# An adapter with a residual and a layer norm on one core: x written ahead of a product, b2 moved between engines, and the order of work set by keys

## The chip, the cores and the metric

The kernel runs on one core of one Trainium2 chip. The metric is the device time of one execution in microseconds (us), the median of several. A core has a TensorE (matmul; the profile lists its weight loads apart as PEld), a VectorE (DVE), a ScalarE (ACT), a GpSimd (POOL) and a SyncE (SP), which here issues DMAs. Each engine works through its own queue in order; semaphores hold one back until another has done its part. SBUF is the working memory, PSUM the memory that TensorE writes, in 8 banks of 128 x 512 float32.

## The reference

128 batches, each with x of 128 x 512 float32 and one id out of 10 that picks its weights:

```python
h = relu(x @ W1[id] + b1[id])            # 128x512 @ 512x128
adapted = h @ W2[id] + b2[id]            # 128x128 @ 128x512
y = x + adapted
normed = (y - mean(y)) * rsqrt(var(y) + 1e-5)
out = x + normed * gamma[id] + beta[id]
```

Everything is float32.

## The kernel before

One batch fills the 128 partitions, with x's 128 rows on them. All of W1 (`w1`), W2 (`w2`), and beta, gamma and b2 spread over the partitions (`beta_b`, `gamma_b`, `b2_b`) lie in SBUF; an id, read into a register by `lid`, picks a slice of 512 columns. For each batch:

- TensorE transposes x in four pieces into `pxT` (`transpose_x`, L271), multiplies by W1 in four steps into `ph` ("down", L294), and by W2 into `py` ("up", L311). A float32 product stands as two matmuls in the profile.
- ScalarE copies `pxT` to `xT` (`copy_xT`, L275), applies relu with b1 (`relu`, L302, `ph` to `hT`), copies the W1 of a coming batch into a tile of its own (`stage_w1`, L262; for batches 0 to 16 a DMA does that by id), and squares y with its sum kept (`square`, L351, followed by a read of the accumulator). Once for each pair of batches it makes the negative means (`scalar_means`, L342) and the first reciprocal root (`deviation`, L361).
- GpSimd adds beta to x (`add_beta`, L288, into the output tile `o`) and b2 to x (`add_b2`, L281, into `r`).
- VectorE adds `r` to `py` in place with the row sums kept (`residual`, L328), refines the root in three small steps a pair (`rstd`, L365, L367, L370), then forms (y - mean) * gamma (`scale`, L394), and times the deviation plus `o` (`finish`, L403). SP stores a pair (`store`, L407).

For 27 of the batches b2 is not added by GpSimd: VectorE adds it to `py` (`vector_b2`, L321) ahead of a residual that reads x itself. For batches 0, 1, 126 and 127 a small matmul adds it.

PSUM: `pxT`, `ph` and the roots have one bank each, `py` has five, used in turn; so the bank of batch b is that of batch b - 5, free after the latter's `finish`. x comes in groups of four batches (`load_x`, four tiles), `r` has four tiles, `o` eight of a pair each.

The order on each engine is the order in which the program calls the steps (`keep` chains each instruction to the one before it on its engine). After a start written out by hand, a loop over i from 3 to 121 calls, in one turn: the transposes of batch i, the adds of GpSimd for batch i - 1, the product down, xT copy and relu around batches i and i - 1, the W1 copy of batch i + 1, the product up of batch i - 2, and VectorE's and ScalarE's statistics for batch i - 3 and the pair before it. The last batches from 121 on (E = B - 5 = 123) are again written out by hand, step for step.

Of the kernel before, what the change touches and what calls it, by code (L numbers as in the profile page):

```python
# [8 lines left out]
FP = mybir.dt.float32  # L9
# [7 lines left out]
P = 128  # L17
# [3 lines left out]
EARLY = 17  # L21
LATE = 17
U = 2


@with_exitstack
def cond_resid_kernel(ctx: ExitStack, tc: tile.TileContext, x, itok, W1, b1, W2, b2, gamma, beta, out):
# [41 lines left out]
    def load_x(g):  # L69
        t = xp.tile([P, G, H], FP, tag="x", name=f"x_{g}")  # L70
        keep(nc.sync.dma_start(out=t, in_=x[g * G : (g + 1) * G].rearrange("b s h -> s b h")))
        xs[g] = t

    def xb(b):
        return xs[b // G][:, b % G, :]
# [64 lines left out]
    def lid(b, engine):  # L140
        g = b // G
        if (g, engine) not in lids:
            loads, vals = nc.values_load_multi_w_load_instructions(  # L143
                lang[0:1, g * G : (g + 1) * G],
                engines=[engine],
                min_val=0,
                max_val=L - 1,
                skip_runtime_bounds_check_because="clamped on the chip to 0..L-1 above",
            )
            for ins in loads:  # L150
                keep(ins)
            lids[g, engine] = vals
        return lids[g, engine][b % G]
# [99 lines left out]
    def b2_by_matmul(b):  # L253
        return b in (0, 1) or b >= B - 2

    def b2_by_vector(b):
        return b in (2, 3, 9, 13, 17, 21) or 24 <= b < B - 8 and (b % 16 in (1, 6, 11) or b % 32 == 30)

    def stage_w1(b):
        w1s[b] = wp.tile([P, KC, A], FP, tag="w1s", name=f"w1s_{b}")  # L260
        src = w1.rearrange("p l k a -> p (l k a)")[:, bass.ds(lid(b, ET.Activation) * (KC * A), KC * A)]
        keep(nc.scalar.copy(w1s[b].rearrange("p k a -> p (k a)"), src))  # L262

    def transpose_x(b):
        pxs[b] = p_x.tile([P, KC, P], FP, tag="xT", name=f"pxT_{b}")
        for k in range(KC):
            if b < EARLY:
                cols = xb(b).rearrange("s (p k) -> s k p", k=KC)[:, k, :]
            else:
                cols = xb(b)[:, k * P : (k + 1) * P]  # L270
            keep(nc.tensor.transpose(pxs[b][:, k, :], cols, ident))  # L271

    def copy_xT(b):
        xT[b] = tp.tile([P, KC, P], FP, tag="xT", name=f"xT_{b}")
        keep(nc.scalar.copy(xT[b], pxs.pop(b)))  # L275

    def add_b2(b):
        if not b2_by_matmul(b) and not b2_by_vector(b):
            rs[b] = rp.tile([P, H], FP, tag="r", name=f"r_{b}")
            v = lid(b, ET.Pool)  # L280
            keep(nc.gpsimd.tensor_tensor(rs[b], xb(b), b2_b[:, bass.ds(v * H, H)], ALU.add))  # L281

    def add_beta(b):
        g, j = divmod(b, 2)
        if j == 0:
            os[g] = op.tile([P, 2, H], FP, tag="o", name=f"o_{g}")
        v = lid(b, ET.Pool)
        keep(nc.gpsimd.tensor_tensor(os[g][:, j, :], xb(b), beta_b[:, bass.ds(v * H, H)], ALU.add))  # L288

    def down(b):  # L290
        phs[b] = p_h.tile([P, P], FP, tag="h", name=f"ph_{b}")
        for k in range(KC):
            keep(
                nc.tensor.matmul(  # L294
                    phs[b], lhsT=w1s[b][:, k, :], rhs=xT[b][:, k, :], start=(k == 0), stop=(k == KC - 1)
                )
            )
        del xT[b], w1s[b]

    def relu(b):  # L300
        hT[b] = tp.tile([P, P], FP, tag="hT", name=f"hT_{b}", bufs=6)
        keep(nc.scalar.activation(hT[b], phs.pop(b), AF.Relu, bias=b1T[:, bass.ds(lid(b, ET.Activation), 1)]))  # L302

    def up(b):
        v = lid(b, ET.PE)
        ys[b] = p_y.tile([P, H], FP, tag="y", name=f"py_{b}")
        m = b2_by_matmul(b)
        if m:
            pick_b = pick[:, bass.ds(v + 2 * L, 1)].to_broadcast([96, P])
            keep(nc.tensor.matmul(ys[b], lhsT=pick_b, rhs=parts[:96, :], start=True, stop=False))  # L310
        keep(nc.tensor.matmul(ys[b], lhsT=hT[b], rhs=w2[:, bass.ds(v * H, H)], start=not m, stop=True))  # L311
        del hT[b]

    def col(tiles, b):

        return tiles[b // 2][:, b % 2 : b % 2 + 1]

    def vector_b2(b):
        if b2_by_vector(b):
            v = lid(b, ET.DVE)  # L320
            keep(nc.vector.tensor_tensor(ys[b], ys[b], b2_b[:, bass.ds(v * H, H)], ALU.add))  # L321

    def residual(b):
        r = rs.pop(b) if b in rs else xb(b)
        if b % 2 == 0:
            sums[b // 2] = st.tile([P, 2], FP, tag="sum", name=f"sum_{b // 2}")
        keep(
            nc.vector.scalar_tensor_tensor(ys[b], ys[b], 1.0, r, ALU.mult, ALU.add, accum_out=col(sums, b))  # L328
        )

    def negative_means(g):
# [12 lines left out]
    def square(b):  # L344

        g, j = divmod(b, 2)
        if j == 0:
            ssqs[g] = st.tile([P, 2], FP, tag="ssq", name=f"ssq_{g}")
        sq = tp.tile([P, H], FP, tag="sq", name=f"sq_{b}")
        keep(  # L350
            nc.scalar.activation(  # L351
                sq, ys[b], AF.Square, bias=col(sums, b), scale=-float(H), accum_out=col(ssqs, b)
            )
        )
# [24 lines left out]
    def deviation(g):  # L379
        root(ssqs[g], of_pair(g)[0])  # L380

    def rstd(g, n):
        t, u = of_pair(g)
        if n < 3:
            newton(n, ssqs[g], t, u)
        else:
            rstds[g] = st.tile([P, 2], FP, tag="rstd", name=f"rstd_{g}")
            newton_3(rstds[g], t, u)
            del ssqs[g], parts_of[g]

    def scale(b):
        v = lid(b, ET.DVE)
        keep(
            nc.vector.scalar_tensor_tensor(  # L394
                ys[b], ys[b], col(nmeans, b), gamma_b[:, bass.ds(v * H, H)], ALU.add, ALU.mult
            )
        )

    def finish(b):
        g, j = divmod(b, 2)  # L400
        o = os[g][:, j, :]
        keep(
            nc.vector.scalar_tensor_tensor(o, ys[b], rstds[g][:, j : j + 1], o, ALU.mult, ALU.add)  # L403
        )
# [4 lines left out]
    def on(b):  # L409
        return 0 <= b < B  # L410
# [48 lines left out]

    def square_of(b):  # L460
        ssqs[-b] = st.tile([P, 1], FP, tag="ssq", name=f"ssq_of_{b}")
        sq = tp.tile([P, H], FP, tag="sq", name=f"sq_{b}")
        keep(nc.scalar.activation(sq, ys[b], AF.Square, bias=col(sums, b), scale=-float(H), accum_out=ssqs[-b]))

    def root_of(b):
# [112 lines left out]
    up(1)  # L578
    x_turn(4)

    turned = 5
    for i in range(3, B - 6):
        b = i - U - 1
        if b == 8 or b > 12 and b % G == 2 and b // G + 3 < NG:
            load_x(5 if b == 8 else b // G + 3)
        up_to = i
        if b <= E:
            if turned <= up_to and on(turned):
                transpose_x(turned)
            add_b2(b + 2)  # L590
            if 4 <= b + 2 <= E:
                add_beta(b + 2)
        for n in range(turned, min(B, up_to) + 1):
            if on(n) and (n > turned or b > E):
                transpose_x(n)
            down(n - 1)
            if on(n):
                copy_xT(n)
            relu(n - 1)
            if on(n + 1) and n + 1 >= FIRST:  # L600
                stage_w1(n + 1)
        turned = max(turned, min(B, up_to) + 1)
        if i - U >= 2 and on(i - U):
            up(i - U)

        g, half = divmod(b, 2)
        p = g - 1
        mine, old = 0 <= p < B // 2, 0 <= p - 1 < B // 2
        if half == 0:
            if on(b):  # L610
                vector_b2(b)
                residual(b)
                square(b)
            if mine:
                scale(2 * p)
                rstd(p, 1)
            if old:
                finish(2 * p - 1)
                store(p - 1)
        else:  # L620
            if on(b):
                vector_b2(b)
            if mine:
                rstd(p, 2)
            if on(b):
                residual(b)
                square(b)
            if mine:
                rstd(p, 3)
                scale(2 * p + 1)  # L630
            if mine:
                finish(2 * p)
        if 0 <= g and b <= E and half == 1:
            scalar_means(g)
            deviation(g)

        for n, engine in ((turned + 2, ET.Activation), (i - U + 3, ET.PE), (b + 1, ET.DVE), (b + 6, ET.Pool)):
            if on(n):
                lid(n, engine)

    lid(E - 3, ET.DVE)
    lid(E + 1, ET.DVE)
# [186 lines left out]
```

## Time and profile before

| | |
|---|---|
| time, median of 3 runs | 303.0 us (302.88 to 303.15) |
| profiled execution: span from first to last instruction | 301.3 us |
| what the median of the runs has above that span | 1.7 us |
| TensorE busy | 293.5 us, 97% |
| VectorE busy | 294.0 us, 98% |
| ScalarE busy | 278.5 us, 92% |
| GpSimd busy | 281.0 us, 93% |
| granted TensorE clock | 1.000 |
| moved by DMA | 78.11 MB, 259 GB/s |

The execution that was profiled has no other time than its span; the runs' times are those of executions as a whole. Busy times are sums of an engine's instructions, with overlaps counted once. Four engines are over 90% busy, so a share alone does not tell which of them sets the pace; that has to be read from the rows in order of time. In a row of the timeline the first number is the start, the second the duration, both in us; rows on one engine overlap, so what an instruction costs its engine is the distance from its start to the next one's start. Matmuls are pipelined, and their ends are modelled.

### The profile page before, as it was taken

To read this page: it belongs to the slowest core of one execution; us is meant where nothing else is said; L and a number is where in the kernel's file an instruction comes from. 1 tells how busy PE (TensorE), PEld (TensorE's weight loads), DVE (VectorE), ACT (ScalarE), POOL (GpSimd) and SP (SyncE) were. 2 spreads that over 40 slices of the span, in tenths; PEclk is the share of its full clock that TensorE was granted. 3 is DMA by queue.
4 is the path that set the end of the run, shared out by engine and by line. 5 is a ranking of instruction groups with operands and counts; after the bars stand their busy time and mean duration, and the time that the engine had idled before them with its cause. 6 is when DMAs were issued, how large, how long until landed. Compare 5 with 4: busy or idle time off the path is not lost.

```text
span 301.3 us, 7022 instructions
## 1 busy us (share of the span) xinstructions
PE 293.5 (97%) x1827; PEld 219.1 (73%) x1827; DVE 294.0 (98%) x785; ACT 278.5 (92%) x770; POOL 281.0 (93%) x236
## 2 busy tenths in 40 slices
PE   7899999999999999999999999999999999999993
PEld 3758787777777777777777777777777777777761
DVE  6989999999999999999999999999999999999996
ACT  5868789999999999999999999999999999999983
POOL 1299998999999999999999999999999999999982
PEclk9999999999999999999999999999999999999999
DMA  6999999996667776766687666668765767782826
GB/s 234 377 390 367 346 321 396 405 337 209 234 229 256 280 235 197 252 242 233 240 281 250 209 209 246 257 231 281 263 204 196 254 232 253 278 271 79 280 89 228
DMA packets 45353, 78.11 MB, mean 259 GB/s; under 512 B 2137, under 2 KB 9316, under 8 KB 45314
## 3 DMA queue, kind: packets, MB, share of 16 engines
q1 hardware_dynamic: 45254, 77.62, 74.9%
q8 instruction: 15, 0.25, 0.3%
q14 instruction: 24, 0.20, 0.2%
q10 hardware_dynamic: 60, 0.05, 0.1%
HBM read 44.11 MB, written 33.55 MB: 258 GB/s over the span
## 4 chain that ended last, share of the span: by engine, by line
PE 87%; DVE 5%; DMA 3%; issue 2%; SPq 1%; POOL 0%; DVEq 0%; POOLq 0%
PE ph L294 35%; PE py L311 35%; PE pxT L271 18%; DMA w<-in_L_cond_W_dram 3%; DVE py L328 1%; DVE o L488 1%; DVE py L394 1%; SPq L161 1%; DVE n L494 0%; SPq L143 0%; DVE rstd_of L370 0%; SPq L88 0%; DVEq L824 0%; DVE part_of L367 0%; DVE shift L434 0%
## 5 line engine op out<-in xcount | busy, mean ns | idle before, releaser
L288 POOL TENSOR_TENSOR o<-x,beta_b 128x512 f32<-128x512 f32 x121 | 158.4, 1331 | 12.8 <-DVE beta_b L247 11.6
L294 PE MATMUL ph<-xT,w1s 128*128 128x128 f32 x1024 | 135.4, 275 | 0.1
L311 PE MATMUL py<-w,hT 128*128 x256 | 131.5, 595 | 0.6 <-DMA w<-in_L_cond_W_dram 0.6
L294 PEld LDWEIGHTS ph<-xT,w1s 128*128 128x128 f32 x1024 | 124.9, 192 | 1.8 <-issue 0.8
L281 POOL TENSOR_TENSOR r<-x,b_b 128x512 f32<-128x512 f32 x92 | 122.7, 1334 | 0.0
L271 PEld LDWEIGHTS pxT<-ident,x 128*128 128x128 f32 x512 | 65.8, 149 | 66.3 <-issue 49.9
L394 DVE SCALAR_TENSOR_TENSOR py<-py,nmean,gamma_b 128x512 f32<-128x512 f32 x124 | 93.2, 752 | 0.0
L403 DVE SCALAR_TENSOR_TENSOR o<-py,rstd,o 128x512 f32<-128x512 f32 x116 | 86.5, 745 | 0.0
L351 ACT ACTIVATE sq<-py,sum 128x512 f32<-128x512 f32 x124 | 85.8, 692 | 0.2 <-DVE rstd L370 0.2
L275 ACT COPY xT<-pxT 128x512 f32<-128x512 f32 x128 | 74.7, 584 | 5.9 <-PE pxT L271 5.8
L271 PE MATMUL pxT<-ident,x 128*128 128x128 f32 x512 | 77.6, 274 | 0.9 <-ACT gamma_b L232 0.7
L328 DVE SCALAR_TENSOR_TENSOR py<-py,r 128x512 f32<-128x512 f32 x97 | 66.7, 688 | 0.1
L262 ACT COPY w1s<-w 128x512 f32 x108 | 66.2, 613 | 0.0
L302 ACT ACTIVATE hT<-ph,b1T 128x128 f32<-128x128 f32 x128 | 46.9, 367 | 8.6 <-PE ph L294 4.0
L311 PEld LDWEIGHTS py<-w,hT 128*128 128x128 f32 x256 | 39.0, 192 | 2.2 <-DMA w<-in_L_cond_W_dram 1.1
L351 ACT ACTIVATION_READ_ACCUMULATOR sq<-py,sum 128x1 f32 x124 | 25.1, 203 | 0.0
L328 DVE SCALAR_TENSOR_TENSOR py<-py,x 128x512 f32<-128x512 f32 x31 | 21.7, 699 | 0.8 <-PE py L311 0.3
L321 DVE TENSOR_TENSOR py<-py,b_b 128x512 f32<-128x512 f32 x27 | 18.6, 689 | 0.8 <-ACT xT L275 0.6
L361 ACT ACTIVATE root<-ssq,eps 128x2 f32<-128x2 f32 x62 | 16.4, 265 | 0.0
L328 DVE DVE_READ_ACCUMULATOR py<-py,r 128x1 f32 x97 | 13.4, 138 | 0.0
L342 ACT ACTIVATE nmean<-sum 128x2 f32<-128x2 f32 x61 | 12.1, 199 | 0.0
L370 DVE SCALAR_TENSOR_TENSOR rstd<-part,root 128x2 f32<-128x2 f32 x62 | 9.2, 149 | 0.0
(73 smaller groups left out, 104.5 us busy)
## 6 DMA issues: line engine op xcount, KB each, us to landing
out_dram<-o SPq DMA_DIRECT2D x62, 512.0 KB, 3.5
x<-in_x_dram SPq DMA_DIRECT2D x27, 1024.0 KB, 6.5
x<-in_x_dram SPq DMA_DIRECT2D x10, 512.0 KB, 6.0
w1s<-in_L_cond_W_dram SPq DMA_DIRECT2D x20, 256.0 KB, 7.7
w<-in_L_cond_W_dram SPq DMA_DIRECT2D x4, 640.0 KB, 8.4
w<-in_L_cond_W_dram SPq DMA_DIRECT2D x1, 1792.0 KB, 10.2
w<-in_L_cond_W_dram SPq DMA_DIRECT2D x1, 768.0 KB, 5.2
out_dram<-o SPq DMA_DIRECT2D x4, 128.0 KB, 1.7
```

Of the source, the lines that this page charges most:

```text
L262: keep(nc.scalar.copy(w1s[b].rearrange("p k a -> p (k a)"), src))
L271: keep(nc.tensor.transpose(pxs[b][:, k, :], cols, ident))
L275: keep(nc.scalar.copy(xT[b], pxs.pop(b)))
L281: keep(nc.gpsimd.tensor_tensor(rs[b], xb(b), b2_b[:, bass.ds(v * H, H)], ALU.add))
L288: keep(nc.gpsimd.tensor_tensor(os[g][:, j, :], xb(b), beta_b[:, bass.ds(v * H, H)], ALU.add))
L294: nc.tensor.matmul(phs[b], lhsT=w1s[b][:, k, :], rhs=xT[b][:, k, :], start=(k == 0), stop=(k == KC - 1))
L302: keep(nc.scalar.activation(hT[b], phs.pop(b), AF.Relu, bias=b1T[:, bass.ds(lid(b, ET.Activation), 1)]))
L311: keep(nc.tensor.matmul(ys[b], lhsT=hT[b], rhs=w2[:, bass.ds(v * H, H)], start=not m, stop=True))
L328: nc.vector.scalar_tensor_tensor(ys[b], ys[b], 1.0, r, ALU.mult, ALU.add, accum_out=col(sums, b))
L351: nc.scalar.activation(sq, ys[b], AF.Square, bias=col(sums, b), scale=-float(H), accum_out=col(ssqs, b))
L394: nc.vector.scalar_tensor_tensor(ys[b], ys[b], col(nmeans, b), gamma_b[:, bass.ds(v * H, H)], ALU.add, ALU.mult)
L403: nc.vector.scalar_tensor_tensor(o, ys[b], rstds[g][:, j : j + 1], o, ALU.mult, ALU.add)
```

## The change

The batches from 27 to 119 get a kind by their number modulo 16 (`KINDS`): 4 of 16 are E, 12 are P.

- P: GpSimd adds b2 to x, as before.
- E ("seeded"): ScalarE copies x into the batch's `py` bank (`seed`), the product up adds to what lies there (`start=False`), and VectorE's residual pass reads b2 in place of x or r. GpSimd does no b2 add.
- `vector_b2` is left for batches 2, 3, 9, 13, 17 and 21 alone.

Of the batches with number 13 modulo 16 from 29 to 109, six in all, W1 comes by a DMA by id (`load_late`) in place of ScalarE's copy.

The loop is replaced by a list: each step of each batch gets a key, in units of one batch, and the steps are called in the order of their keys. On ScalarE the W1 copy of a coming batch now mostly stands ahead of the relu, and a seed ahead of the xT copy of two batches later; on VectorE the last two of the three small steps follow each other directly in the middle. `EDGE` holds the keys of pairs outside the middle, `PAIR` those inside. `hT` has 5 tiles in place of 6, the squares' scratch tile 1 in place of 2. TensorE's order of matmuls, the start and the end written by hand stay.

```diff
+MIDDLE = 27
+TURNED = 19
+LAST = 8
+KINDS = 'EPPPPPEPPPEPEPPP'
+TURNS = 'TTTTTTTTTTTTTwTT'
+SEEDED = 'E'
+ON_GPSIMD = 'P'
+BATCH = dict(copy=0.09, r=0.59, beta=-0.52, relu=1.24, w1=-0.83, up=2.43, load=-4.76, r_late=-1.39)
+SEED = {'E': 1.88}
+PAIR = dict(stat=0.27, square=0.28, means=1.67, root=1.89, scale0=2.48, n1=2.77, n2=3.135, n3=3.19, scale1=3.02, end0=3.44, end1=4.28)
+EDGE = dict(stat=0.53, square=0.74, means=1.74, root=2.0, scale0=3.04, n1=2.84, n2=3.345, n3=3.7, scale1=4.07, end0=4.09, end1=4.71)
...
+    def kind(b):
+        return KINDS[b % len(KINDS)] if MIDDLE <= b < B - LAST else "-"
+
+    def turn(b):
+        return TURNS[b % len(TURNS)] if TURNED <= b < B - LAST - 2 else "-"
+
+    def seeded(b):
+        return kind(b) in SEEDED
...
     def b2_by_vector(b):
-        return b in (2, 3, 9, 13, 17, 21) or 24 <= b < B - 8 and (b % 16 in (1, 6, 11) or b % 32 == 30)
+        return kind(b) == "-" and (b in (2, 3, 9, 13, 17, 21) or 24 <= b < B - 8 and (b % 16 in (1, 6, 11) or b % 32 == 30))
...
+    def seed(b):
+        ys[b] = p_y.tile([P, H], FP, tag="y", name=f"py_{b}")
+        keep(nc.scalar.copy(ys[b], rs.pop(b) if b in rs else xb(b)))
...
-        hT[b] = tp.tile([P, P], FP, tag="hT", name=f"hT_{b}", bufs=6)
+        hT[b] = tp.tile([P, P], FP, tag="hT", name=f"hT_{b}", bufs=5)
...
     def up(b):
         v = lid(b, ET.PE)
+        if seeded(b):
+            cols = w2[:, bass.ds(v * H, H)]
+            keep(nc.tensor.matmul(ys[b], lhsT=hT[b], rhs=cols, start=False, stop=True, skip_group_check=True))
+            del hT[b]
+            return
...
     def residual(b):
-        r = rs.pop(b) if b in rs else xb(b)
...
+        if seeded(b):
+            r = b2_b[:, bass.ds(lid(b, ET.DVE) * H, H)]
+        else:
+            r = rs.pop(b) if b in rs else xb(b)
...
-        sq = tp.tile([P, H], FP, tag="sq", name=f"sq_{b}")
+        sq = tp.tile([P, H], FP, tag="sq", name=f"sq_{b}", bufs=1)
...
-    for i in range(3, B - 6):
...
+    for b in range(B):
+        if b >= 20 and b % G == 0:
+            at((11 if b == 20 else b - 7) - 0.01, load_x, b // G)
+        if b >= 3:
+            for n, engine in ((b + 5, ET.Activation), (b + 5, ET.PE), (b + 2, ET.DVE), (b + 6, ET.Pool)):
+                if on(n):
+                    at(b + 0.99, lid, n, engine)
+        if turn(b) in "Fw":
+            at(b + BATCH["load"] - 1, lid, b, ET.SP)
+            at(b + BATCH["load"], load_late, b)
+        if 5 <= b <= E - 2:
+            at(b, transpose_x, b)
+            at(b + BATCH["copy"], copy_xT, b)
+        if 4 <= b <= E - 3:
+            add_to = b + (BATCH["r"] if seeded(b) else BATCH["r_late"])
+            at(add_to, add_b2, b)
+            at(b + BATCH["beta"], add_beta, b)
+            at(b + 1.1, down, b)
+            at(b + BATCH["relu"], relu, b)
+        if seeded(b):
+            at(b + SEED[kind(b)], seed, b)
+        if FIRST <= b <= E - 1 and turn(b) not in "Fw":
+            at(b + BATCH["w1"], stage_w1, b)
+        if 2 <= b <= E - 4:
+            at(b + BATCH["up"], up, b)
...
+    for g in range(E // 2 - 1):
+        b = 2 * g
+        when = EDGE if "-" in (kind(b), kind(b + 2)) else PAIR
+        for j in (0, 1):
+            at_pair(g, j + when["stat"] - 0.01, vector_b2, b + j)
+            at_pair(g, j + when["stat"], residual, b + j)
+            at_pair(g, j + when["square"], square, b + j)
+        at_pair(g, when["means"], scalar_means, g)
+        at_pair(g, when["root"], deviation, g)
+        for n in (1, 2, 3):
+            at_pair(g, when[f"n{n}"], rstd, g, n)
+        for j in (0, 1):
+            at_pair(g, when[f"scale{j}"], scale, b + j)
+            at_pair(g, when[f"end{j}"], finish, b + j)
+        at_pair(g, when["end1"] + 0.001, store, g)
+
+    for _, _, step, args in sorted(plan, key=lambda step: step[:2]):
+        step(*args)
```

A step of a pair g gets the key 2g + 3 plus the number in `PAIR` or `EDGE` (`at_pair`); steps that the hand-written end does itself are left out of the list.

More of the change, by code (lines that the diff above doesn't have):

```diff
@@ L254, in b2_by_matmul, with b2_on_gpsimd, sum_of @@
         return b in (0, 1) or b >= B - 2
-    def b2_by_vector(b):
-        return b in (2, 3, 9, 13, 17, 21) or 24 <= b < B - 8 and (b % 16 in (1, 6, 11) or b % 32 == 30)
+    def kind(b):
[4 more added lines that the diff above has]
+        return kind(b) in SEEDED
+    def b2_on_gpsimd(b):
+        return kind(b) in ON_GPSIMD or kind(b) == "-" and not b2_by_matmul(b) and not b2_by_vector(b)
+    def b2_by_vector(b):
+        return kind(b) == "-" and (b in (2, 3, 9, 13, 17, 21) or 24 <= b < B - 8 and (b % 16 in (1, 6, 11) or b % 32 == 30))
+    def sum_of(b):
+        if b // 2 not in sums:
+            sums[b // 2] = st.tile([P, 2], FP, tag="sum", name=f"sum_{b // 2}")
+        return col(sums, b)
+    def seed(b):
+        ys[b] = p_y.tile([P, H], FP, tag="y", name=f"py_{b}")
+        keep(nc.scalar.copy(ys[b], rs.pop(b) if b in rs else xb(b)))
     def stage_w1(b):
@@ L277, in add_b2 @@
     def add_b2(b):
-        if not b2_by_matmul(b) and not b2_by_vector(b):
+        if b2_on_gpsimd(b):
             rs[b] = rp.tile([P, H], FP, tag="r", name=f"r_{b}")
@@ L323, in residual @@
     def residual(b):
-        r = rs.pop(b) if b in rs else xb(b)
-        if b % 2 == 0:
-            sums[b // 2] = st.tile([P, 2], FP, tag="sum", name=f"sum_{b // 2}")
+        if seeded(b):
+            r = b2_b[:, bass.ds(lid(b, ET.DVE) * H, H)]
+        else:
+            r = rs.pop(b) if b in rs else xb(b)
         keep(
-            nc.vector.scalar_tensor_tensor(ys[b], ys[b], 1.0, r, ALU.mult, ALU.add, accum_out=col(sums, b))
+            nc.vector.scalar_tensor_tensor(ys[b], ys[b], 1.0, r, ALU.mult, ALU.add, accum_out=sum_of(b))
         )
@@ L461, in square_of @@
         ssqs[-b] = st.tile([P, 1], FP, tag="ssq", name=f"ssq_of_{b}")
-        sq = tp.tile([P, H], FP, tag="sq", name=f"sq_{b}")
+        sq = tp.tile([P, H], FP, tag="sq", name=f"sq_{b}", bufs=1)
         keep(nc.scalar.activation(sq, ys[b], AF.Square, bias=col(sums, b), scale=-float(H), accum_out=ssqs[-b]))
@@ L579, in cond_resid_kernel @@
     x_turn(4)
-    turned = 5
-    for i in range(3, B - 6):
[L583 to L639, printed above, removed]
@@ new lines, in cond_resid_kernel, with at @@
+    plan = []
+    def at(when, step, *args):
+        plan.append((when, len(plan), step, args))
+    for b in range(B):
[23 more added lines that the diff above has]
+            at(b + BATCH["up"], up, b)
@@ new lines, in cond_resid_kernel, with at_pair @@
+    begun = [(step, n) for n in (E - 7, E - 6, E - 5) for step in (vector_b2, residual, square)]
+    begun += [(scalar_means, E // 2 - 3), (deviation, E // 2 - 3), (scale, E - 7), (rstd, E // 2 - 3, 1)]
+    def at_pair(g, when, step, *args):
+        if g < E // 2 - 3 or (step, *args) in begun:
+            at(2 * g + 3 + when, step, *args)
+    for g in range(E // 2 - 1):
[13 more added lines that the diff above has]
+        at_pair(g, when["end1"] + 0.001, store, g)
```

## Prediction

> **What bounds the kernel now.** I read the page's first part, then the chain that ended last, then the stages, then single rows of one steady stretch.
>
> ```profile
> span 301.3 us, 7022 instructions
> PE 293.5 (97%) x1827; PEld 219.1 (73%) x1827; DVE 294.0 (98%) x785; ACT 278.5 (92%) x770; POOL 281.0 (93%) x236
> PE 87%; DVE 5%; DMA 3%; issue 2%; SPq 1%; POOL 0%; DVEq 0%; POOLq 0%
> ```
>
> The chain is 87% TensorE, yet VectorE is as busy as TensorE. The stages (columns: PE, PEld, DVE, ACT, POOL busy, clock, DMA share, GB/s) say the same.
>
> ```profile
> 140.00:160.00 20.00, 20.00 (x130) 15.24 (x129) 19.96 (x54) 19.56 (x55) 20.00 (x18) 1.00 0.61 211
> 240.00:260.00 20.00, 20.00 (x131) 15.26 (x130) 19.96 (x54) 19.65 (x56) 20.00 (x17) 1.00 0.76 246
> ```
>
> Busy shares cannot tell which of three full engines leads, so I look at whether TensorE ever loses time. In the chain, `ph` is the product down of one batch:
>
> ```profile
> 47.19 0.89 PE ph L294 x8
> 91.90 0.99 PE py L311 x2
> 162.14 0.99 PE py L311 x2
> 232.37 0.99 PE py L311 x2
> 276.32 0.86 PE py L311 x2
> 277.19 0.44 PE pxT L271 x4
> 277.62 0.89 PE ph L294 x8
> ```
>
> Between the first and last row lie 105 batches: 230.43 us. Three products up take 0.99 instead of 0.86, together 0.39 us; the rest is (230.43 - 0.39)/105 = 2.191 us a batch. That is exactly 0.44 (transposes) + 0.89 (down) + 0.86 (up). So from 47 to 278 us TensorE is a solid row of matmuls without a gap, and nothing done on another engine can shorten it. One batch of it, with its weight loads and ScalarE's row for the copy that one of them waits for:
>
> ```profile
> 154.07 0.60 PE L271 MATMUL pxT<-ident,x 128*128 128x128 f32 x4
> 155.40 1.02 PE L311 MATMUL py<-w,hT 128*128 x2
> 153.65 0.14 PEld L271 LDWEIGHTS pxT<-ident,x 128*128 128x128 f32 x1 [0.24 <-ACT xT L275]
> 154.40 0.97 PEld L294 LDWEIGHTS ph<-xT,w1s 128*128 128x128 f32 x8
> 155.29 0.30 PEld L311 LDWEIGHTS py<-w,hT 128*128 128x128 f32 x2
> ```
>
> Counted from the start of the transposes (a "slot"), down wants its first weights at 0.33 us, up at 1.22 us.
>
> **The change, part by part.** The matmuls, their number and their order on TensorE stay; only register loads shift by a slot. Costs are therefore loads on three side engines, set against 16 x 2.191 = 35.06 us that TensorE needs for 16 batches. The changed middle is 93 batches, 5.8 such periods.
>
> *VectorE loses the b2 adds* (21 of the 27; from batch 27 on none is left).
>
> ```profile
> 150.33 0.69 DVE L328 SCALAR_TENSOR_TENSOR py<-py,r 128x512 f32<-128x512 f32 x1
> 152.34 0.69 DVE L321 TENSOR_TENSOR py<-py,b_b 128x512 f32<-128x512 f32 x1
> 153.06 0.70 DVE L328 SCALAR_TENSOR_TENSOR py<-py,x 128x512 f32<-128x512 f32 x1
> 155.13 0.69 DVE L328 SCALAR_TENSOR_TENSOR py<-py,r 128x512 f32<-128x512 f32 x1
> ```
>
> From 150.33 to 155.13 VectorE does two batches' work with one add: 4.80 us, of which the add takes 153.06 - 152.34 = 0.72. Without it a pair is 4.08, against 4.38 on TensorE. Before, 3.5 adds in 16 batches made it 8 x 4.08 + 3.5 x 0.72 = 35.2: full. After, 32.6. The last two Newton steps, kept apart before by a wide operation, now stand back to back; the second waits for the first, between nothing and one whole such operation (0.15 us) a pair, at most 1.2 in 16 batches. Hidden: VectorE keeps at least 1.2 us free. Saving 0.72 x 21 = 15 us here is worth nothing in the middle, because TensorE covers it.
>
> *GpSimd* does 12 adds of b2 in 16 batches instead of 12.5.
>
> ```profile
> 152.34 2.57 POOL L288 TENSOR_TENSOR o<-x,beta_b 128x512 f32<-128x512 f32 x2
> 154.81 1.33 POOL L281 TENSOR_TENSOR r<-x,b_b 128x512 f32<-128x512 f32 x1
> ```
>
> Two operations span 154.81 - 152.34 = 2.47, so 1.235 each: 28.5 of them took 35.2, 28 take 34.6. Off the path.
>
> *ScalarE gains 4 seeds and loses 1 copy of W1 in 16 batches.*
>
> ```profile
> 152.00 0.69 ACT L351 ACTIVATE sq<-py,sum 128x512 f32<-128x512 f32 x1
> 152.58 0.20 ACT L351 ACTIVATION_READ_ACCUMULATOR sq<-py,sum 128x1 f32 x1
> 152.67 0.20 ACT L342 ACTIVATE nmean<-sum 128x2 f32<-128x2 f32 x1
> 152.81 0.27 ACT L361 ACTIVATE root<-ssq,eps 128x2 f32<-128x2 f32 x1
> 153.01 0.58 ACT L275 COPY xT<-pxT 128x512 f32<-128x512 f32 x1
> 153.49 0.37 ACT L302 ACTIVATE hT<-ph,b1T 128x128 f32<-128x128 f32 x1
> 153.75 0.62 ACT L262 COPY w1s<-w 128x512 f32 x1
> 154.25 0.70 ACT L351 ACTIVATE sq<-py,sum 128x512 f32<-128x512 f32 x1
> ```
>
> From start to start: square 0.58, its read 0.09, mean 0.14, root 0.20, xT 0.48, relu 0.26, W1 0.50. A pair is 2 x 1.91 + 0.34 = 4.16, 16 batches 33.3; free are 1.76. No row shows a copy from SBUF into PSUM. Nearest is the W1 copy, the same 512 columns from SBUF: 0.50. Below, the xT copy, 0.48; above, a copy that overlaps with nothing, 0.62. I take 0.50: added 4 x 0.50 - 0.50 = 1.50, which fits by 0.26. At 0.62 it is 1.98 and lacks 0.22. The break-even is a seed of 0.56.
> The Trainium skill (ScalarE: Activation LUTs, "Step-by-step: what each stage is for") holds PSUM to be the faster destination for ScalarE, without a figure; the rows here show copies out of PSUM alone. By that rule the seed would lie under the 0.50 and the sum would fit by more.
>
> *A fit on average must also hold slot by slot*, because ScalarE works strictly in order. The new order puts the W1 copy ahead of relu and the seed ahead of the xT copy. ScalarE then runs forward until xT waits for its transposes (end 0.60, so 0.64): xT 0.64, W1 1.12, relu 1.62, square 1.88, mean, root; next slot xT 0.70, relu 1.68, and it is free again at 0.42 of the third. There a seed goes: 0.42 to 1.04. The weights of its product up are due at 1.22; a weight load starts 0.06 after ScalarE's row (153.01 + 0.58, then 153.65), so the limit is 1.16. Everything behind moves by 0.28 net: relu of the following slot ends at 1.96 + 0.37 = 2.33, limit 2.19 + 0.33 - 0.06 = 2.46, as the single PSUM bank of `ph` must be empty for the next down. A seed's delay is worked off at 0.22 a pair. Seeds stand at places 0, 6, 10, 12 of 16; between 10 and 12 the W1 copy left out (place 13) gives 0.50 back. The carry-over is at most 0.06, and the margins shrink to 0.06 and 0.07 us. So no stall, but hardly any cover: queued behind a late seed are xT, W1 and relu, and TensorE waits for all of them.
>
> *The bank.* A seed takes its `py` bank 0.55 slot ahead of the product. It needs the finish of five batches earlier: planned at 1.28 slots after the batch's own number, the seed at 1.88, so 0.60 x 2.19 = 1.3 us apart. Hidden by that.
>
> *W1 by id*, 6 DMAs of 256 KB on SP's queue:
>
> ```profile
> w1s<-in_L_cond_W_dram SPq DMA_DIRECT2D x20, 256.0 KB, 7.7
> ```
>
> Placed 4.76 slots ahead and wanted 1.1 slots after, 12.8 us for a landing of 7.7: 5.1 us cover for a store waiting in front of it. The load of x behind it in the queue moves by one issue. Cost nothing.
>
> *The end.* The code behind batch 122's start is the same; VectorE arrives there earlier.
>
> ```profile
> 276.16 1.02 PE L311 MATMUL py<-w,hT 128*128 x2
> 277.83 0.69 DVE L328 SCALAR_TENSOR_TENSOR py<-py,r 128x512 f32<-128x512 f32 x1
> 278.35 1.02 PE L311 MATMUL py<-w,hT 128*128 x2
> 280.70 0.59 PE L311 MATMUL py<-w,hT 128*128 x1
> 292.52 1.11 PE L311 MATMUL py<-w,hT 128*128 x2
> 294.01 0.69 DVE L328 SCALAR_TENSOR_TENSOR py<-py,x 128x512 f32<-128x512 f32 x1
> ```
>
> Before, VectorE is 277.83 - 277.18 = 0.65 late here, as batch 118 still had an add; ScalarE's chain behind it makes one product up 280.70 - 278.35 - 2.19 = 0.16 late. That goes. After the last product up (end 293.63) VectorE starts 0.38 late; at most that goes too. Gain between 0 and 0.54; I take 0.2, since the end's own VectorE work has no idle time.
>
> *Sum:* 301.3 - 0.2 + 0.1 for an occasional missed margin (its bounds: 0, and rival one) = 301.2 of span. The median of the runs, 303.0, lies 1.7 above this execution's span, so 302.9.
>
> **Rivals.** One, slower: ScalarE has not the time. Place: relu, hence the `ph` bank, hence the next down. Price: with a seed of 0.62, 0.22 x 5.8 = 1.3 us, 304.2; if every one of the 23 seeds misses its margin by 0.1, 2.3 us, 305.2. It decides from 0.56 a seed. For it: margins of 0.06. Against: every ScalarE row overlaps the one behind it by about 0.1.
>
> Two, slower: the seed waits for the bank. VectorE must be 1.3 us late; then xT is stuck behind it. Some 0.2 us for 23 seeds is 4.6: 307.5. Against: VectorE has time to spare after the change.
>
> Three, slower by far: gaps cost clock. The stages show 1.00 throughout, beside stalls of 0.13. One half-speed stretch as long as a slot and a half (3.3 us) a period would lose 1.7 x 5.8 = 10 us: 313. The Trainium skill (TensorE: Matmul & The Clock Gate, "A second HAM failure mode: psum-queue depth-cycling") tells of micro-idling between PSUM groups that lets the clock oscillate; by it this rival would come, the trace so far disagrees.
>
> Four, faster by more than 0.2%: the whole 0.54 at the end and the three 0.13 vanish: 302.1. Against: the 0.13 come every 70 us, 32 batches, whatever the side engines do.
>
> That the change moves work which TensorE hides anyway is the forecast itself.
>
> **How the numbers follow.** About 0.2% (0.6 us) is what can be told from no change. Forecast 0.58; rival one 0.25, two 0.06, three 0.01, four 0.10. Below 302.4 is more than 0.6 gained: 0.10; above 303.6 0.32, most of it rival one. The range takes in rival one's bounds: 302.3 to 305.3; the forecast's own is 302.4 to 303.4.
>
> **What would show it.** Right: `ph` rows still 2.19 apart in the middle; VectorE about 18.6 to 19.2 of 20 us; ScalarE 19.8 or more; seed rows at 0.50 to the next start; no TensorE or weight-load wait on ScalarE that costs a slot. Wrong: seeded batches with slots over 2.19, weight loads of `py` or `ph` waiting for the seed or relu, seeds idle before VectorE's finish. The forecast falls if a seed takes over 0.56 or if its wait holds up xT.

## The result, and the profile after

The changed kernel takes 304.17 us (median of 5 runs, 303.94 to 304.29), the kernel before on the same chip 302.99 (302.88 to 303.15). The ratio is 1.0039, with a 95% interval of 1.0028 to 1.0050: slower by 0.4%. The profiled execution has a span of 302.5 us and a time of 304.29, against a span of 301.3 before.

The page of the changed kernel (span, busy times, the chain that ended last), and two stages of its middle (columns as in the prediction):

```profile
span 302.5 us, 7080 instructions
PE 294.3 (97%) x1827; PEld 219.4 (73%) x1827; DVE 287.9 (95%) x764; ACT 283.1 (94%) x787; POOL 278.7 (92%) x234
ACT 55%; issue 16%; DVE 13%; PE 7%; DMA 5%; ACTq 2%; SPq 1%; DVEq 0%; POOL 0%; POOLq 0%
```

```profile
140.00:160.00 20.00, 20.00 (x131) 15.25 (x129) 19.47 (x50) 20.00 (x58) 20.00 (x17) 1.00 0.71 244
240.00:260.00 20.00, 20.00 (x128) 15.12 (x127) 19.36 (x51) 20.00 (x58) 20.00 (x18) 1.00 0.79 258
```

The chain has gone over from TensorE (87%) to ScalarE (55%), and ScalarE is now full, 20.00 of 20. Yet TensorE is as full as before in both stages. The share of the chain says which engine arrives last, and here that may be by a few hundredths of a microsecond; it does not say how much is lost. So I set the start of each product up against that of the same batch before and noted where the distance changes:

| where | us | what TensorE waits for |
|---|---|---|
| start of the program | -0.08 | differs from execution to execution: -0.26 to +0.22 in the kernels below, which all begin alike |
| batch 4 (23.6 us) | +0.15 | ScalarE's second square waits for its first |
| batches 19 to 24 (57 to 69 us) | +1.01 | `py` bank of the batch five earlier, VectorE's `finish` |
| 11 batches of the middle, 0.02 to 0.04 each | +0.38 | five times a seed, six times a relu, both on ScalarE |
| batches 35, 67, 99 | -0.39 | the three stalls of 0.13 are gone |
| batch 121 | -0.16 | the late product up is gone |
| batch 125 | +0.03 | |
| last product up to the end | +0.25 | the last stores |

The sum is 1.19, of 1.2 in the spans. Five sixths of it arise in six batches ahead of the middle, where the change has no seed at all. The waits there, from 50 to 72 us (engine and line, what ended the wait, us in all, times, longest): two groups of the changed kernel, and then all of the weight loads' groups of the kernel before in the same stretch:

```profile
PEld py L348 <- DVE o L441: 0.8, 3, 0.3
DVE py L432 <- issue: 1.2, 3, 0.5
```

```profile
PEld pxT L271 <- issue: 4.1, 15, 0.3
PEld pxT L271 <- ACT xT L275: 1.2, 5, 0.2
```

TensorE's weights of a product up wait for a `finish` (L441), and VectorE itself idles three times ahead of a `scale` (L432) without any engine to wait for. One such place in the timeline of the changed kernel, and the register load by which VectorE's queue gets four ids (its view: minimum, median and maximum in ns, then its start):

```profile
58.90 0.69 DVE L366 SCALAR_TENSOR_TENSOR py<-py,r 128x512 f32<-128x512 f32 x1
59.51 0.14 DVE L366 DVE_READ_ACCUMULATOR py<-py,r 128x1 f32 x1
59.51 0.15 DVE L408 SCALAR_TENSOR_TENSOR rstd<-part,root 128x2 f32<-128x2 f32 x1
60.16 0.76 DVE L432 SCALAR_TENSOR_TENSOR py<-py,nmean,gamma_b 128x512 f32<-128x512 f32 x1 [0.50 <-issue]
60.83 0.74 DVE L441 SCALAR_TENSOR_TENSOR o<-py,rstd,o 128x512 f32<-128x512 f32 x1
```

```profile
L154 DVEq TENSOR_LOAD <-lang x1: 927/927/927, 59.0 to 59.0; - x1
```

The load is not counted as busy time, but it holds VectorE's queue from 59.0 to 60.0. The last operation handed to the engine ahead of it ends at 59.66 (59.51 + 0.15), and the `scale` starts 0.2 us after the load's end. This `scale` is that of batch 17, the load brings the ids of batches 24 to 27: the `scale` has no use for them, it only stands behind the load in the queue. Before, the load stood behind `finish`, so VectorE had a further 0.7 us of work already handed over while the load ran; the same stretch of the kernel before has no gap:

```profile
58.79 0.15 DVE L370 SCALAR_TENSOR_TENSOR rstd<-part,root 128x2 f32<-128x2 f32 x1
58.86 0.75 DVE L394 SCALAR_TENSOR_TENSOR py<-py,nmean,gamma_b 128x512 f32<-128x512 f32 x1
59.52 0.75 DVE L403 SCALAR_TENSOR_TENSOR o<-py,rstd,o 128x512 f32<-128x512 f32 x1
```

Its load in this stretch took 0.34 us alone. But the one ahead of it took 0.90, and VectorE does not idle behind that either:

```profile
L143 DVEq TENSOR_LOAD <-lang x1: 903/903/903, 50.2 to 50.2; - x1
```

What follows on TensorE in the changed kernel, the weights of three products up:

```profile
56.98 0.30 PEld L348 LDWEIGHTS py<-w,hT 128*128 128x128 f32 x2 [0.25 <-DVE o L441]
61.62 0.30 PEld L348 LDWEIGHTS py<-w,hT 128*128 128x128 f32 x2 [0.19 <-DVE o L441]
66.42 0.30 PEld L348 LDWEIGHTS py<-w,hT 128*128 128x128 f32 x2 [0.34 <-DVE o L441]
```

### The profile page after: what moved, and what is told of

It reads as the page before. It is cut to its first block, busy times and chain, and to the rows that moved or that the text cites. A ratio compares the mean times of both kernels' runs of the same rounds, so it can differ in the third digit from the quotient of the medians.

```text
span 302.5 us, 7080 instructions
## 1 busy us (share of the span) xinstructions
PE 294.3 (97%) x1827; PEld 219.4 (73%) x1827; DVE 287.9 (95%) x764; ACT 283.1 (94%) x787; POOL 278.7 (92%) x234
## 4 chain that ended last, share of the span: by engine, by line
ACT 55%; issue 16%; DVE 13%; PE 7%; DMA 5%; ACTq 2%; SPq 1%; DVEq 0%; POOL 0%; POOLq 0%
ACT sq L389 20%; ACT xT L307 14%; ACT w1s L294 10%; ACT hT L334 8%; DVE py L366 4%; DMA w<-in_L_cond_W_dram 3%; PE py L348 3%; DVE o L441 2%; DVE py L432 2%; PE ph L326 2%; DMA out_dram<-o 2%; ACT nmean L380 1%; DVE o L526 1%; PE pxT L303 1%; ACTq L154 1%
## 5 line engine op out<-in xcount | busy, mean ns | idle before, releaser
L320 POOL TENSOR_TENSOR o<-x,beta_b 128x512 f32<-128x512 f32 x121 | 154.0, 1286 | 12.7 <-DVE beta_b L258 11.6
L313 POOL TENSOR_TENSOR r<-x,b_b 128x512 f32<-128x512 f32 x90 | 115.8, 1287 | 1.0 <-DVE py L366 1.0
L432 DVE SCALAR_TENSOR_TENSOR py<-py,nmean,gamma_b 128x512 f32<-128x512 f32 x124 | 91.9, 751 | 1.6 <-issue 1.5
L441 DVE SCALAR_TENSOR_TENSOR o<-py,rstd,o 128x512 f32<-128x512 f32 x116 | 86.5, 746 | 0.0
L294 ACT COPY w1s<-w 128x512 f32 x102 | 63.7, 625 | 0.0
L334 ACT ACTIVATE hT<-ph,b1T 128x128 f32<-128x128 f32 x128 | 48.1, 376 | 3.8 <-PE ph L326 3.4
L348 PEld LDWEIGHTS py<-w,hT 128*128 128x128 f32 x210 | 32.0, 192 | 2.5 <-DMA w<-in_L_cond_W_dram 0.8
L389 ACT ACTIVATION_READ_ACCUMULATOR sq<-py,sum 128x1 f32 x124 | 26.4, 213 | 0.0
L366 DVE SCALAR_TENSOR_TENSOR py<-py,b_b 128x512 f32<-128x512 f32 x23 | 16.1, 698 | 1.0
L289 ACT COPY py<-x 128x512 f32<-128x512 f32 x23 | 13.8, 600 | 0.0
L380 ACT ACTIVATE nmean<-sum 128x2 f32<-128x2 f32 x61 | 13.4, 220 | 0.0
```

The lines of the kernel that those rows point to most:

```text
L432: nc.vector.scalar_tensor_tensor(ys[b], ys[b], col(nmeans, b), gamma_b[:, bass.ds(v * H, H)], ALU.add, ALU.mult)
```

## The experiments

**The load put back.** In the changed kernel, VectorE's load alone gets a later key, which sets it behind a `finish` again, up to batch 30 (`LIDS`).

```diff
-                    at(b + 0.99, lid, n, engine)
+                    at(b + (1.2 if engine == ET.DVE and b <= LIDS else 0.99), lid, n, engine)
```

> The changed kernel with one thing moved: up to batch 30 VectorE's register load of a group's ids stands behind a finish again, as in the kernel before, and not in front of a scale. Theory (the loads in front of scale leave VectorE idle up to 0.5 us, it was full there, so finish and with it the py bank come late): the stalls of TensorE between 55 and 70 us, 1.0 us in all, are gone, 303.1 to 303.3. Rival (the new order itself, finish ahead of scale on VectorE and the W1 copy ahead of relu on ScalarE, costs it): 304.2 as the changed kernel.

Measured: 303.43 us (303.21 to 303.86), 1.0016 [1.0007, 1.0025] of before; span 301.5. All steps at batches 19 to 24 are gone, the others stay. In the same stretch, this kernel's load at 59.0 is even longer, but neither VectorE nor a product up waits: the `finish` ahead of the load runs to 60.30, past the load's end at 60.1.

```profile
L155 DVEq TENSOR_LOAD <-lang x1: 1069/1069/1069, 59.0 to 59.0; - x1
```

```profile
55.00:70.00 15.00, 15.00 (x99) 11.54 (x98) 14.97 (x39) 14.84 (x43) 15.00 (x13) 1.00 0.99 357
```

The same stage of the changed kernel:

```profile
55.00:70.00 15.00, 14.78 (x90) 10.76 (x89) 14.24 (x39) 13.84 (x40) 15.00 (x13) 1.00 0.95 342
```

TensorE has 90 matmuls in place of 99 there, and VectorE idles 0.76 of the 15 us. So the place of one register load makes 1.0 us between the two profiled executions, 0.7 between the medians. The median lies 0.13 above what was expected, because the expectation took the 1.0 of a profile off the median: the profiled execution of the changed kernel is the longest of its five (304.29), that of this kernel the shortest of its eleven (303.21).

**The rival for the same stretch.** There the change also puts the copy of W1 ahead of the relu on ScalarE; here it stands behind the relu again, and the load stays where the change has it.

```diff
-            at(b + BATCH["w1"], stage_w1, b)
+            at(b + (-0.7 if b < MIDDLE else BATCH["w1"]), stage_w1, b)
```

> The changed kernel with ScalarE's relu back ahead of the W1 copy for batches below 27; VectorE's register loads stay where the change put them. Theory of the register loads: no difference, 304.0 to 304.3. Rival of ScalarE's new order outside the middle: the 1.0 us comes back, 303.2.

Measured: 304.37 us (303.75 to 304.63), 1.0037 [1.0023, 1.0050]; the steps at batches 19 to 24 are all there (0.99 in sum). The order of the W1 copy and the relu is not the cause.

**The load moved in the kernel before.** Nothing but VectorE's load, in front of the `scale` of the odd batch, in a kernel without keys, seeds or new order.

```diff
+                if on(b + 1):
+                    lid(b + 1, ET.DVE)
                 scale(2 * p + 1)
```

> The kernel before with this one part of the change alone: VectorE's register load of each group moved from behind a finish to in front of the scale of an odd batch. VectorE is full there throughout, with 31 such loads, of 0.34 to 0.95 us each, of which some 0.45 is covered. Theory: TensorE pays for them, about 0.2 to 0.25 us a load, 304.5 to 311. Rival: 303.0, if a register load is hidden anyway.

Measured: 304.31 us (304.14 to 304.64), 1.0048 [1.0034, 1.0062], just under the 304.5 expected: the move alone costs 1.3 us. That this is close to the 1.18 of the change is chance, for the steps stand elsewhere, from batch 19 to batch 99. It is far less than the 24 loads of the middle could have cost, because there most of them were short. VectorE's waits ahead of a `scale`, and the load between 80 and 250 us, first in this kernel, then in the kernel before:

```profile
DVE py L394 <- issue: 1.2, 3, 0.6
```

```profile
L143 DVEq TENSOR_LOAD <-lang x19: 340/343/560, 85.4 to 244.3; - x19
```

```profile
L143 DVEq TENSOR_LOAD <-lang x19: 594/630/656, 85.7 to 243.8; - x19
```

A load of 0.34 us ends while the residual ahead of it still runs. Of the three waits, two stand behind long loads: 0.56 us behind one of 1.00 at 49.4, 0.41 behind one of 0.56 at 217.2. TensorE's steps at batches 19 and 20 (0.32) follow the first, those at 93 to 99 (0.49) come behind the second. The third, 0.26, stands behind a load of 0.34, and no step follows it. Some 0.4 us of smaller steps between batches 24 and 67 have no idle VectorE next to them; their cause is open.

**Keys without seeds, and the load's place in them.** Two kernels: the changed kernel without seeds and without W1 by id (all 27 adds of b2 stay on VectorE, the keys of the edge hold everywhere), once with the load behind `finish` (the key 1.2 as above, for all batches), once where the change puts it.

```diff
-MIDDLE = 27
+MIDDLE = 200
-TURNED = 19
+TURNED = 200
```

> The changed kernel without seeds and without the six loads of W1 by id: VectorE adds b2 for the same 27 batches as before, the order comes from the keys, and VectorE's register load stands behind a finish everywhere. My ledger, from 303.0 before: the one scratch tile of the squares +0.15 at the start, the three 0.13 stalls and the late product up of batch 121 stay, no steps of 0.04 in the middle, the end as before, as no load is added: 303.1, between 302.9 and 303.3. Rival, the order by keys costs by itself (its small VectorE steps stand together): above 303.6.

> The same with VectorE's register load where the change puts it, in front of a scale of an odd batch, all the way through. VectorE then has its 27 adds and no time to spare in the middle. If the b2 adds that the seeds take away are what covers those loads, the time lies above the run with the loads put back by at least 1.2 us, as in the kernel before with the loads moved: 304.4 or more, up to 309 if each of some 24 loads costs the 0.25 us that the four of the changed kernel cost at batches 13 to 25. If the loads cost something at the start alone, the time is that of the changed kernel, 304.1, with no stall behind batch 27.

Measured: 303.41 us (303.16 to 304.04; 1.0012 [1.0003, 1.0021]) with the load behind `finish`, 312.21 us (311.98 to 312.59; 1.0302 [1.0288, 1.0316]) with the load in front of `scale`. The first lies 0.1 above its range, the second above the 309 expected at most. One instruction's place is worth 8.8 us. The waits of the slower one, its load between 80 and 250 us, a stage of the middle, and one place in it:

```profile
PEld py L348 <- DVE o L441: 6.6, 20, 0.6
DVE py L432 <- issue: 6.6, 21, 0.7
```

```profile
L154 DVEq TENSOR_LOAD <-lang x18: 652/698/732, 86.8 to 241.8; - x18
```

```profile
140.00:160.00 20.00, 19.80 (x125) 14.79 (x124) 19.57 (x53) 19.20 (x53) 20.00 (x17) 1.00 0.74 256
```

```profile
159.92 0.15 DVE L408 SCALAR_TENSOR_TENSOR rstd<-part,root 128x2 f32<-128x2 f32 x1
160.35 0.76 DVE L432 SCALAR_TENSOR_TENSOR py<-py,nmean,gamma_b 128x512 f32<-128x512 f32 x1 [0.28 <-issue]
```

Here nearly all the loads are long, 21 of 32 leave VectorE idle, and VectorE with its 27 adds has no time to make it good; 20 products up wait for it. In the middle of the changed kernel this does not happen, though its loads there are long too (median 0.61). Two things differ: the keys of the middle (`PAIR`) put the load behind a `finish`, and VectorE has some 0.6 of 20 us to spare. These two runs do not separate the one from the other.

The kernel with the load behind `finish` shows what the seeds are worth, with the six loads and the middle's keys that belong to them: with VectorE's load put back, the kernel takes 303.43 with them and 303.41 without, so nothing. Without seeds, the three stalls of the kernel before stay, and are longer; in the chain, the product up of batch 35 takes 1.06 and not 0.86.

```profile
91.79 1.06 PE py L349 x2
```

**Twice the seeds.** With the load put back, every even batch of the middle is seeded: 46 seeds for 23.

```diff
-KINDS = 'EPPPPPEPPPEPEPPP'
+KINDS = 'EPEPEPEPEPEPEPEP'
```

> e1 with 8 of 16 batches seeded in place of 4 (every even one in the middle). Theory (ScalarE's time bounds the middle from there on): 33.3 + 8 x 0.52 - 0.50 = 37.0 us of ScalarE in 16 batches against 35.06 of TensorE, 1.9 more, in 5.8 periods 11 us: 313 to 316. Rival: seeds are hidden as the adds of VectorE were, 303.4.

Measured, one run: 315.15 us; span 313.4, 11.9 above the 301.5 with 23 seeds. ScalarE is the bound now, so the price of a seed can be read off: 11.9/23 = 0.52 us. A stage, and the group of weights that wait for a seed between 60 and 280 us:

```profile
140.00:160.00 20.00, 20.00 (x126) 14.94 (x124) 18.65 (x52) 20.00 (x57) 15.82 (x13) 1.00 0.74 259
```

```profile
PEld py L341 <- ACT py L290: 6.0, 32, 0.2
```

TensorE stops for 0.1 to 0.23 us in most batches of the middle here, and its granted clock stays 1.00.

**Less for ScalarE.** With the load put back, W1 comes by id for four batches of 16 (places 3, 9, 13, 15), 25 DMAs in all, 19 more than in the changed kernel.

```diff
-TURNS = 'TTTTTTTTTTTTTwTT'
+TURNS = 'TTTwTTTTTwTTTwTw'
```

> As e1, and W1 by id for 4 of 16 batches (places 3, 9, 13, 15) in place of 1, so that each seed on ScalarE is paid with a W1 copy left out. Theory: the stalls of 0.035 us, two in 16 batches, that seeds and late relus leave in the middle (0.4 us in all) go too: 302.6 to 302.9, below both kernels. Rival: the 18 DMAs more of 256 KB each hold up loads of x, 303.5 or more.

Measured: 304.31 us (304.07 to 305.04), 1.0053 [1.0039, 1.0067]: missed. The eleven small steps of the middle are gone, as expected, but one step of 1.25 has come, at the product up of batch 18. Its stretch (52 to 58 us):

```profile
PEld ph L327 <- ACT xT L308: 1.2, 1, 1.2
PE ph L327 <- DMA w1s<-in_L_cond_W_dram: 1.0, 1, 1.0
```

The product down of batch 19 waits for its W1, which is still in transit. The DMA was issued at 45.25 us, behind two stores in SP's queue, and 8.3 us ahead of the time at which the product could have started (53.5), not the 12.8 of its key; the product starts 9.4 us after the issue (54.7), and the DMA engines have little room here (a share of 1.06 from 50 to 58 us of this run). The 5.1 us of cover that I worked out for a load in the middle do not hold at 55 us.

**The squares' scratch tile.** With the load put back, two tiles for the squares, as before the change.

```diff
-        sq = tp.tile([P, H], FP, tag="sq", name=f"sq_{b}", bufs=1)
+        sq = tp.tile([P, H], FP, tag="sq", name=f"sq_{b}", bufs=2)
```

> e1, and the scratch tile of the squares has two buffers again in place of one. Theory: with one buffer the second square waits for ScalarE's own first one, which costs 0.15 us at the start, where two squares stand side by side (product up of batch 4), and nowhere else: 0.15 us less than e1, about 303.3. Rival: what e1 has above the kernel before comes from the seeds, then the same as e1, 303.4.

Measured: 303.20 us (302.93 to 303.31), 1.0004 [0.9995, 1.0013]. The step at batch 4 is gone. What it was: the first two squares' rows on ScalarE, of the changed kernel and of the kernel before.

```profile
20.18 0.20 ACT L389 ACTIVATION_READ_ACCUMULATOR sq<-py,sum 128x1 f32 x1
20.42 0.69 ACT L389 ACTIVATE sq<-py,sum 128x512 f32<-128x512 f32 x1
```

```profile
20.26 0.20 ACT L351 ACTIVATION_READ_ACCUMULATOR sq<-py,sum 128x1 f32 x1
20.35 0.69 ACT L351 ACTIVATE sq<-py,sum 128x512 f32<-128x512 f32 x1
```

From the read to the next square it is 0.24 with one tile and 0.09 with two: with one, the second square waits on a semaphore that ScalarE itself raises when its read behind the first square ends (20.18 + 0.20).

**Better versions.** Both have the load put back and two tiles for the squares. One takes W1 by id for two batches more (47 and 111), eight in all; the other for 16 batches: 29, and from 41 on the places 9, 13 and 15 of 16.

```diff
+        return "w" if 29 <= b < B - LAST - 2 and b % 16 == 13 or b in (47, 111) else "-"
```

```diff
+        return "w" if b % 16 in (9, 13, 15) and (b == 29 or 41 <= b < B - LAST - 2) else "-"
```

> e8, and W1 by id for 8 batches in place of 6 (47 and 111 are added). The DMAs' 8 semaphores are dealt out in turn and the program waits for them at its end in a fixed order; with 6 loads more the last two stores hold semaphores that are not the last ones waited for, with 8 more they hold the same as before. Theory: from the last product up to the end 8.8 us again in place of 9.06, 303.0. Rival: the number of loads does not matter to the end, 303.3 as e8.

> e8, and W1 by id for 16 batches (places 9, 13 and 15 of 16, from 41 on, and 29), so that ScalarE has time for its seeds and the end's semaphores stand as before. Theory: the end as in e10, and no stall of 0.035 us in the middle: 302.5 to 302.7, below both kernels. Rival: the loads hold up something, 303.0 or more.

Measured: 302.59 us (302.51 to 303.07), 0.9989 [0.9980, 0.9998], with eight loads, and 302.48 us (302.24 to 304.42), 0.9989 [0.9977, 1.0002], with 16. So both are about 0.1% below the kernel before, which is less than the 0.2% that I hold a measurement of this kernel can tell. The one with eight loads came out 0.4 lower than expected, the one with 16 where it was expected. With 16 the small steps of the middle are gone altogether, and the last product up starts 0.41 earlier than before; with eight loads it is 0.19 earlier. From there to the end the one with 16 loses 0.29 again, the one with eight nothing (0.01). The kernels that load no W1 by id in the middle lose nothing there either (0.02 at most, three runs), those with six 0.23 to 0.30, the one with 25 0.40: it is these loads, and not the seeds or the keys, that change the end. The last stores on SP's queue (start and time in which they are issued), of the kernel before, the changed one, the one with eight loads and the one with 16 (spans 301.3, 302.5, 301.1 and 301.2 us):

```profile
295.30 3.77 SPq L520 DMA_DIRECT2D out_dram<-o  x6
```

```profile
296.21 3.76 SPq L558 DMA_DIRECT2D out_dram<-o  x6
```

```profile
295.12 3.77 SPq L559 DMA_DIRECT2D out_dram<-o  x6
```

```profile
294.89 3.77 SPq L559 DMA_DIRECT2D out_dram<-o  x6
```

From the last issue to the end of the span it is 2.23 before (301.3 - 295.30 - 3.77), 2.53 after, 2.21 with eight loads and 2.54 with 16. The 0.25 to 0.3 at the end thus come behind all the computing, in the landing of the last stores and the waits for it. SP waits for eight semaphores of DMAs in a fixed order there, which the DMAs take in turn; six loads more shift which of them the last two stores hold, and eight or 16 shift them around, back to where they were. In the trace of the changed kernel two more waits of 0.06 us thus stand behind that for the last store, 0.12 in all. The rest is the landing: SP's wait for the last store ends 1.38 us after its issue before, 1.55 after, 1.39 with eight loads and 1.68 with 16, where the stores hold the same semaphores as before. Why the landing differs is open.

## Why the prediction was wrong

I forecast no change, 302.9 us with 302.4 to 303.4 as that case's own range; measured are 304.17. That lies in the range of all cases (302.3 to 305.3) and beside the 304.2 that rival one has for a seed of 0.62, but by chance: a seed takes 0.52, and 1.01 of the 1.19 us arise where there are no seeds.

*The step that failed* is half a sentence at the head of the change's parts: "only register loads shift by a slot". They were costed at nothing, and no cover was named for them. The runs have in its place: VectorE's load, of 0.34 to 0.95 us in the changed kernel, has gone from behind a `finish` to in front of a `scale`, where the work handed over ahead of it lasts 0.6 us from the load's start (59.04 to 59.66) and not 1.3 (59.03 to 60.30 with the load put back). Put back, 0.74 us of the 1.18 are gone; moved alone in the kernel before, where nearly all the loads are then short, it costs 1.3; in the kernel without seeds, where nearly all are long, 8.8. The prediction showed "VectorE keeps at least 1.2 us free" for the middle only. The cover was gone ahead of the middle, where the change leaves VectorE's adds for batches 13, 17 and 21 and uses the edge's keys; I worked out no slot of that stretch. The trace of before had the cost, a median of 0.63 us in the middle and 0.90 at 50.2; it would have been enough to ask what hides that. The Trainium skill (DMA: Bandwidth & Descriptors, "Latency and other measured facts") gives a floor of about 600 ns for such a load; most of the loads here agree (median 0.61 after), but 0.34 us is the median where the load was moved in the kernel before, so here it is no floor.

*Smaller terms left out or off in size.* The one scratch tile of the squares was told in the change and not costed at all: 0.15. That W1 by id would "Cost nothing" holds in the middle, where none of the six loads was waited for; but the end became 0.25 longer with six loads and not with eight, and 25 loads cost 1.25 at batch 18. "0.1 for an occasional missed margin" was 0.38. VectorE is busy 19.3 to 19.5 of 20 us in the middle from 100 us on, above the 18.6 to 19.2 that were to be seen; its busy time fell by 6.1 us in all (294.0 to 287.9), and not by the 15 of the adds.

*A statement that was wrong.* Against rival four I held that the stalls of 0.13 come every 32 batches "whatever the side engines do". They are gone in the changed kernel and in each run with 23 seeds. They stand at batches 35, 67 and 99, five behind 30, 62 and 94, and these are the ones to which the kernel before gives its one additional VectorE add in 32 batches; five is the number of `py` banks. The rows of before have the wait: the `finish` of batch 30 ends at 91.71, and the weights of the product up of batch 35 start 0.06 behind it.

```profile
90.96 0.75 DVE L403 SCALAR_TENSOR_TENSOR o<-py,rstd,o 128x512 f32<-128x512 f32 x1
```

```profile
91.77 0.30 PEld L311 LDWEIGHTS py<-w,hT 128*128 128x128 f32 x2
```

Without seeds, where these adds stay, the stalls are there, 0.2 long in the chain above. So VectorE's saved time was worth 0.39, not nothing, and a regular stall was a sign of its load.

*What was right.* TensorE's 2.191 us a batch is the floor: no version of the middle went below it, and with 15 us of adds taken off VectorE the gain in the middle is the 0.39 just told. The price of a seed, 0.50 taken from the W1 copy, with 0.56 as break-even: 0.52, from the run with 46 seeds and from the rows. First the group of all 23 seeds, then one of them in ScalarE's order, then the weights of its product up:

```profile
L289 ACT COPY py<-x 128x512 f32<-128x512 f32 x23 | 13.8, 600 | 0.0
```

```profile
106.02 0.61 ACT L294 COPY w1s<-w 128x512 f32 x1
106.53 0.37 ACT L334 ACTIVATE hT<-ph,b1T 128x128 f32<-128x128 f32 x1
107.45 0.60 ACT L289 COPY py<-x 128x512 f32<-128x512 f32 x1
107.97 0.60 ACT L307 COPY xT<-pxT 128x512 f32<-128x512 f32 x1
```

```profile
107.17 0.97 PEld L326 LDWEIGHTS ph<-xT,w1s 128*128 128x128 f32 x8
108.11 0.30 PEld L340 LDWEIGHTS py<-w,hT 128*128 128x128 f32 x2
```

From start to start the seed takes 0.52, the W1 copy in the batch before 0.51. The Trainium skill (ScalarE: Activation LUTs, "Step-by-step: what each stage is for") has PSUM as the faster destination; from start to start these rows show no such gain.

*Rival one* had the right places and too high a price. The two margins of 0.06 and 0.07 were the ones that gave: the weights of the product up start 0.94 behind those of down here and 0.89 before (155.29 - 154.40), so the seed is 0.05 late at place 10; the relu, once in 16 batches, holds down up by 0.02 to 0.04. This is less than 0.1 in 16 batches, and not 0.22 in 16 or 0.1 for each of 23 seeds. It did not add up because the seeds do fit on average, as the sum had it.

*Rival two* did not occur: the seeds' group above has 0.0 idle before it. *Rival three* did not either: with a stall in nearly every batch, in the run with 46 seeds, the clock stayed 1.00. *Rival four* got its three stalls and, of the end's 0.54, 0.16; it was outweighed elsewhere.

## What to carry to other kernels

Where an order is changed, list also what is not busy time: register loads, waits of an engine for itself, the order of the last waits; and ask of each what runs on the engine meanwhile, in every part of the program and not in its steady middle alone. Here a register load was free where the work handed over ahead of it lasted longer than the load (1.3 us), and not where it lasted 0.6. For a stall that recurs with a period, look first at what has that period in the code.

## What was unexpected

The same register load, with the same operations around it on VectorE, takes 0.34 us in nearly all places of one kernel (340/343/560) and 0.70 in those of another (652/698/732). By this a wrong place costs 1.3 us or 8.8. What sets its time was not settled; the number of ids and the tile they come from are the same. Another engine's load at the same time does not decide it: in the kernel before, the load at 76.9 us took 0.64 with none beside it, the one at 85.7 took 0.62 with GpSimd's beside it.

A square that writes the same scratch tile as the one ahead of it on ScalarE started 0.15 us later than with a second tile, although nobody reads that tile.
